# Token layers and last outputs of a scan network, put into one program order of rounds

## The chip, the cores and the metric

The kernel runs on one core of one Trainium2 chip. The metric is the device time of one execution, in microseconds (us). Five engines run at the same time, each with its own queue: TensorE (PE, matmuls and transposes into PSUM), VectorE (DVE), ScalarE (ACT), GpSimd (POOL), and SyncE (SP), which here only issues DMA transfers. They are synchronised by semaphores.

## What is computed

Four images of 64 x 64 positions (L = 4096 tokens) with 96 channels pass through four layers, all in float32 unless the layer quantises:

```python
# layers 0 and 1: selective scan over an image, four directions
xz = x @ in_proj_w.T;  xp, z = split(xz)
xc = silu(depthwise_conv3x3(xp) + conv_b)
# for each of 4 directions: delta, B, C from xc;  h = exp(delta*A)*h + delta*u*B;  y = C.h + D*u
y = layernorm(sum of the directions) * silu(z)
x = x + y @ out_proj_w.T
# layers 2 and 3: on tokens
x = x + attention(layernorm(x))    # no softmax: (q k^T) v, then @ Wff + bff
x = x + ffn(layernorm(x))          # 96 -> 384 -> 96, relu, fp8 (e5m2) products, fp16 accumulation rounding
```

Because the attention has no softmax, the kernel computes it as one 97 x 97 Gram matrix of the normalised tokens (with a column of ones), a chain of four small products that ends in a 97 x 96 matrix, and one product of the tokens with that matrix.

## The kernel before, in words

**Scans.** A scan layer treats the images in two pairs, so there are four units (layer 0 pair 0, layer 0 pair 1, layer 1 pair 0, layer 1 pair 1). A unit is a stage between scans (`between_scans`) and a scan (`PairScan.run`). The scan fills nearly all of the time. The stage between scans runs the input half of the next unit (projection, convolution, `Inputs`) together with the output half of the unit before (layer norm, gate, output projection, `Outputs`); the first stage has inputs only. It goes in beats, with `fill()` between the parts of a beat handing out pieces of the convolution to DVE, PE and POOL by `CONVS` and `SHARES`. `beginnings` is a generator that makes the first projection and first step sizes of the scan that follows; from beat 4 (first stage) or 8 (joined stages) on, four of its pieces are taken at the end of a beat. These stages and the scans use `InOrder`, a wrapper that fixes the order of compute instructions on each engine to the order in which the program writes them.

**Last outputs and token layers.** After the last scan, `token_layers` has two jobs: the `Outputs` of the last unit (16 groups of 256 positions for images 2 and 3, `one_by_one`), and the two token layers of all four images. Images 0 and 1 are already complete in DRAM and are loaded into `tok0` and `tok1` at once; `tok2` and `tok3` are loaded when the outputs are done.

- An output group g is loaded (`zt`, `xr`, three `ys` transfers), measured on DVE (`ystats`, `ymv`), turned into scale factors by a power on POOL (`ln_ve`, `ln_rs`) and a product on DVE (`shift`), normalised on ACT (`ys`), transposed on PE (`pt`), scaled back on ACT (`gt`), gated on DVE, projected on PE (`po`), copied on ACT (`xo`) and stored. All nine steps of a group are written one after the other. Loads have three buffers.
- A token norm (`token_norm`) takes statistics of 32 tiles of 128 tokens on DVE (`tstats`), combines them, takes the power -0.5 on POOL (`tn_ve`, `tn_rs`), forms `tshift` on DVE and applies scale and shift, three tiles of four on ACT and the fourth on POOL (`tn`).
- Attention: for each of 8 groups of 512 tokens, four matmuls into `gram`, four transposes (`tnps`) and an ACT copy to `tnt`; then the chain of small products; then for each group four matmuls (`ops`) and an addition to the tokens on DVE.
- ffn: for each of 8 groups, four transposes and a copy to fp8 (`xq`), three matmuls (`hps`), each followed by a copy to fp16 on ACT (`h`), bias and relu on DVE (`hb`) and a cast to fp8 on POOL (`hq`); then twelve matmuls (`ops`), a copy on ACT (`o`) and two additions on DVE.

Each image is a Python generator that yields between groups; a loop takes one step of the outputs and one step of every started image in turn, and image b may start at turn 13 b. In this stage the instructions are written through `tc.nc` and not through `InOrder`: the compiler's scheduler, which has a priority by the order of writing and its own estimate of durations, decides each engine's order. SP's order is the scheduler's before and after the change. PSUM is shared by tags with two buffers each: `tp` (transposes), `mm` (hidden products and the outputs' `pt`), `o` (outer products and the outputs' `po`).

Of the kernel before, what the change touches and what calls it, by code (L numbers as in the profile page):

```python
# [38 lines left out]
NT = L // 128  # L39
HID = 4 * C  # L40
# [23 lines left out]
def rstd_of(nc, pool, var, shape, tag, half):  # L64

    ve = pool.tile(shape, F32, name=f"{tag}_ve")
    nc.gpsimd.tensor_scalar(ve, var, EPS, None, ALU.add)
    rs = pool.tile(shape, F32, name=f"{tag}_rs")
    nc.gpsimd.tensor_tensor(rs, ve, half, ALU.pow)
    return rs  # L70
# [56 lines left out]
def between_scans(tc, cst, ident, half, pn, u, before, scan, after):  # L127

    with ExitStack() as stage:
# [16 lines left out]
        for beat in range(-LEAD, BEATS + 1):  # L146
# [4 lines left out]
            def fill():  # L151
                if beat < BEATS:
                    for one in convs:
                        one.go(ready)
# [18 lines left out]
            if now:  # L173
                outs.turn(beat)
            fill()
# [11 lines left out]
            if beat >= BEGIN[joint]:  # L187
                for _ in range(4):
                    next(beginnings, None)
# [18 lines left out]
    False: {'vector': ((0, 0, 16), (2, 0, 16), (0, 16, 16), (2, 16, 16), (0, 32, 16), (2, 32, 16), (2, 48, 16), (0, 48, 16)), 'tensor': ((1, 0, 8), (1, 8, 8), (1, 16, 8), (1, 24, 8), (1, 32, 8), (1, 40, 8), (1, 48, 8), (1, 56, 8))},  # L208
# [149 lines left out]
class Outputs:  # L358

    def __init__(self, nc, tc, stage, cst, ident, half, pn, layer, pr, pp, turned="pt", summed="po"):  # L360
# [8 lines left out]
        self.loaded, self.scaled, self.gated, self.sums = {}, {}, {}, {}  # L369
# [51 lines left out]
    def turn(self, g):  # L421
        nc, par, (_, _, ys) = self.nc, self.layer.par, self.loaded[g]
        self.gated[g] = gt = self.p2.tile([128, 3, 2, 128], F32, name="gt", bufs=2)
        for s, js, firsts in ((0, slice(0, 2), (0, 256)), (1, slice(2, 3), (128,))):
            pt = self.pp.tile([128, len(firsts), 2, 128], F32, name="pt", tag=self.turned)
            for j, first in enumerate(firsts):
                for t in range(2):
                    nc.tensor.transpose(pt[:, j, t], ys[:, t, first : first + 128], self.ident)
            nc.scalar.activation(
                gt[:, js], pt, AF.Identity, bias=par[:, s, P_NB : P_NB + 1], scale=par[:, s, P_NW : P_NW + 1]  # L430
            )
# [45 lines left out]
    def one_by_one(self):  # L477
        for g in range(BEATS):
            self.load(g)
            self.measure(g)  # L480
            self.scale(g)
            self.shift(g)
            self.normalise(g)
            self.turn(g)
            self.gate(g)
            self.project(g)
            self.store(g)
            yield
        self.close()
# [369 lines left out]
def token_norm(nc, pool, half, t, tn):  # L859

    stats = pool.tile([128, NT, 6], F32, name="tstats")
    for j in range(NT):
        nc.vector.bn_stats(stats[:, j], t[:, j])
        if j % 8 == 7:
            yield

    (m0, q0), (m1, q1) = ((stats[:, :, i], stats[:, :, i + 1]) for i in (1, 4))

    def small(name):
        return pool.tile([128, NT], F32, name=name)  # L870

    mean2, dev, var = small("tmean2"), small("tdev"), small("tvar")
    nc.vector.tensor_tensor(mean2, m0, m1, ALU.add)
    nc.vector.tensor_tensor(dev, m0, m1, ALU.subtract)
    nc.vector.scalar_tensor_tensor(dev, dev, 0.25, dev, ALU.mult, ALU.mult)
    nc.vector.tensor_tensor(var, q0, q1, ALU.add)
    nc.vector.scalar_tensor_tensor(var, var, 1.0 / C, dev, ALU.mult, ALU.add)
    rs = rstd_of(nc, pool, var, [128, NT], "tn", half)
    shift = small("tshift")
    nc.vector.scalar_tensor_tensor(shift, mean2, -0.5, rs, ALU.mult, ALU.mult)  # L880
    yield
    for j in range(NT):
        scale, bias = rs[:, j : j + 1], shift[:, j : j + 1]
        if j % 4 == 3:
            nc.gpsimd.tensor_scalar(tn[:, j, :C], t[:, j], scale, bias, ALU.mult, ALU.add)
        else:
            nc.scalar.activation(tn[:, j, :C], t[:, j], AF.Identity, bias=bias, scale=scale)
        if j % 8 == 7:
            yield

def turn_tokens(nc, pp, ident, tn, g, out):

    n = out.shape[0]
    ps = pp.tile([n, 512], F32, name="tnps", tag="tp")
    for j in range(4):
        nc.tensor.transpose(ps[:, 128 * j : 128 * j + 128], tn[:, 4 * g + j, :n], ident)
    nc.scalar.activation(out[:, 512 * g : 512 * g + 512], ps, AF.Copy, saturate=False)
# [8 lines left out]
def attention(nc, pool, pp, cst, ident, half, t, w):  # L906

    def product(a, b, name):

        ps = pp.tile([a.shape[1], b.shape[1]], F32, name=name, tag="small", bufs=1)  # L910
        nc.tensor.matmul(ps, a, b, start=True, stop=True)
        return ps

    def kept(ps, name):
        to = pool.tile(list(ps.shape), F32, name=name)
        nc.vector.tensor_copy(to, ps)
        return to

    tn = pool.tile([128, NT, C + 1], F32, name="tn", bufs=3)
    nc.gpsimd.memset(tn[:, :, C : C + 1], 1.0)  # L920
    yield from token_norm(nc, pool, half, t, tn)
    gram = pp.tile([C + 1, C + 1], F32, name="gram", bufs=1)
    tnt = pool.tile([C + 1, L], F32, name="tnt")
    for g in range(NT // 4):
        for j in range(4 * g, 4 * g + 4):
            nc.tensor.matmul(gram, tn[:, j], tn[:, j], start=(j == 0), stop=(j == NT - 1))
        turn_tokens(nc, pp, ident, tn, g, tnt)
        yield
    gk = kept(product(kept(gram, "gram_s"), w["wkv"][:, :C], "gkps"), "gk")
    vk = product(w["wkv"][:, C:], gk, "vkps")  # L930

    heads = pool.tile([C, C], F32, name="heads")
    nc.vector.tensor_tensor(heads, cst["heads"], vk, ALU.mult)
    rest = kept(product(heads, w["Wff"], "hps"), "rest")
    whole = pool.tile([C + 1, C], F32, name="whole")
    nc.vector.tensor_tensor(whole, w["bff"], product(w["wq"], rest, "wps"), ALU.add)
    yield
    for g in range(NT // 4):
        po = pp.tile([128, 4, C], F32, name="ops", tag="o")
        for j in range(4):  # L940
            at = 512 * g + 128 * j
            nc.tensor.matmul(po[:, j], tnt[:, at : at + 128], whole, start=True, stop=True)
        tg = t[:, 4 * g : 4 * g + 4]
        nc.vector.tensor_tensor(tg, tg, po, ALU.add)
        yield

def ffn_weights(nc, pool, w, n):

    def quantised(shape, src, name, back=False):
        raw = pool.tile(shape, F32, name=f"{name}{n}")  # L950
        nc.sync.dma_start(out=raw, in_=src)
        q = pool.tile(shape, E5M2, name=f"{name}q{n}")
        nc.vector.tensor_copy(q, raw, saturate=False)
        if back:
            nc.vector.tensor_copy(raw, q)
            return raw
        return q

    nh = HID // 128
    return (  # L960
        quantised([C, HID], w["W1"], "w1"),
        quantised([128, nh, C], w["W2"].rearrange("(k p) c -> p k c", p=128), "w2"),
        quantised([128, nh], w["b1"], "b1", back=True),
        quantised([128, 1, C], w["b2"].unsqueeze(0).partition_broadcast(128), "b2", back=True),
    )

def ffn(nc, pool, pp, ident, half, t, w, out=None):

    nh = HID // 128
    w1, w2, b1, b2 = w  # L970
    tn = pool.tile([128, NT, C + 1], F32, name="tn", bufs=3)
    yield from token_norm(nc, pool, half, t, tn)
    xq = pool.tile([C, L], E5M2, name="xq")
    for c in range(L // 512):
        turn_tokens(nc, pp, ident, tn, c, xq)
        yield
        cols = slice(512 * c, 512 * c + 512)
        hq = pool.tile([128, nh, 512], E5M2, name="hq")
        for k in range(nh):
            ps = pp.tile([128, 512], F32, name="hps", tag="mm")  # L980
            nc.tensor.matmul(ps, w1[:, 128 * k : 128 * k + 128], xq[:, cols], start=True, stop=True)
            h = pool.tile([128, 512], F16, name="h16")
            nc.scalar.copy(h, ps)
            hb = pool.tile([128, 512], F16, name="hb16")
            nc.vector.tensor_scalar(hb, h, b1[:, k : k + 1], 0.0, ALU.add, ALU.max)
            nc.gpsimd.tensor_copy(hq[:, k], hb, saturate=False)
        po = pp.tile([128, 4, C], F32, name="ops", tag="o")
# [5 lines left out]
        o = pool.tile([128, 4, C], F16, name="o16")  # L993
        nc.scalar.copy(o, po)
        ob = pool.tile([128, 4, C], F16, name="ob16")
        nc.vector.tensor_tensor(ob, o, b2.to_broadcast([128, 4, C]), ALU.add)
        tg = t[:, 4 * c : 4 * c + 4]
        nc.vector.tensor_tensor(tg, tg, ob, ALU.add)
        yield
# [200 lines left out]
```

## Time and profile before

| | |
|---|---|
| median of 3 runs | 10563.6 us (10562.44 to 10565.32) |
| the profiled execution: its own time, its span | 10567.09 us, 10565.3 us |
| last scan instructions on DVE and POOL | end at about 9918 and 9921 us |
| last-outputs and token stage | from about 9922 us to the end |
| its outputs: first statistics, last `xo` copy | 9955.5 us, 10061.8 us |
| busy over the span: PE, DVE, ACT, POOL | 76%, 91%, 84%, 88% |
| instructions of the span | 142182 |

The profile is one execution, recorded by the hardware profiler; times in it are counted from the span's start. A line of a group of instructions has the code line, engine, operation, output<-inputs, tile shapes and count, then the busy time, the mean duration in ns of one, and how long the engine stood idle just before them and for what. Many lines carry L60, the line of the wrapper `InOrder`; the tiles tell what they are. "PEclk" is the granted share of TensorE's full clock.

### The profile page before, as it was taken

How to read it: one execution, taken by the hardware profiler on the slowest of the kernel's cores; microseconds unless marked ns; L12 is line 12 of the kernel's file. 1: busy time of each engine (PE TensorE's matmuls, PEld its weight loads, DVE VectorE, ACT ScalarE, POOL GpSimd, SP SyncE). 2: the span in 40 equal slices, each digit the busy share in tenths (PEclk: the TensorE clock that was granted, in tenths of full speed). 3: DMA queues.
4: the chain of work that ended last, by engine and by line, in shares of the span. 5: the costliest groups of instructions: out<-in, count | busy, mean ns of one | idle time of the engine just before them, and what ended most of it. 6: DMA issues, size and time to landing. Idle time of an engine off the chain costs nothing.

```text
span 10565.3 us, 142182 instructions
## 1 busy us (share of the span) xinstructions
PE 8004.7 (76%) x47518; PEld 5948.7 (56%) x47518; DVE 9628.9 (91%) x6714; ACT 8827.3 (84%) x18798; POOL 9337.2 (88%) x5482
## 2 busy tenths in 40 slices
PE   7777777777777777777777777777877777777666
PEld 4655555554555555555455555555555555555554
DVE  7999999998999999998999999999899999999755
ACT  6888888887888888888888888888788888888756
POOL 3999999998999999998899999999799999999645
PEclk9889898988888889898889888888888998898877
DMA  4677777776667777777567777777566777777600
GB/s 138 202 215 219 218 217 219 221 219 173 206 212 212 217 218 219 219 218 215 169 208 215 214 215 221 223 215 220 172 207 210 215 218 216 218 219 219 197 22 25
DMA packets 903380, 2117.25 MB, mean 200 GB/s; under 512 B 330326, under 2 KB 639896, under 8 KB 704920
## 3 DMA queue, kind: packets, MB, share of 16 engines
q1 hardware_dynamic: 902648, 2108.15, 68.0%
q8 instruction: 378, 6.19, 0.3%
q14 instruction: 354, 2.90, 0.1%
HBM read 1946.42 MB, written 161.48 MB: 200 GB/s over the span
## 4 chain that ended last, share of the span: by engine, by line
ACT 34%; PE 18%; issue 18%; DVE 17%; POOL 10%; DMA 1%; SPq 0%; DVEq 0%; POOLq 0%; ACTq 0%
ACT x L60 15%; ACT da L60 12%; DVE h L60 10%; PE yp L60 6%; POOL h L60 6%; PE bp L60 5%; DVE bp L60 4%; ACT bp L60 2%; DVE u L60 1%; PE xps L60 1%; POOL dbu L60 1%; PE dps L60 1%; ACT L60 1%; PE dups L60 1%; DMA cb<-crow 1%
## 5 line engine op out<-in xcount | busy, mean ns | idle before, releaser
L60 POOL TENSOR_TENSOR h<-h,cb 128x1024 f32<-128x1024 f32 x3072 | 7194.5, 2366 | 231.3 <-issue 61.2
L60 DVE TENSOR_TENSOR_SCAN h<-da,last,bp 128x1024 f32<-128x1024 f32 x2064 | 4736.6, 2335 | 146.0 <-PE bp L60 22.4
L60 ACT ACTIVATE x<-dut,bt 128x128 f32<-128x128 f32 x12288 | 3495.0, 370 | 1.2 <-PE bp L60 1.1
L60 PE MATMUL yp<-ident,h 128*128 128x128 f32 x24576 | 3365.4, 297 | 10.2 <-POOL h L60 10.2
L60 PEld LDWEIGHTS yp<-ident,h 128*128 128x128 f32 x24576 | 3191.2, 156 | 126.8 <-issue 76.9
L60 ACT ACTIVATE da<-delta,amat 128x1024 f32<-128x1024 f32 x2752 | 3059.7, 1138 | 99.0 <-DVE h L60 97.0
L60 PE MATMUL bp<-ident,x 128*128 128x128 f32 x10240 | 1673.3, 315 | 1292.5 <-DVE h L60 950.6
L60 PEld LDWEIGHTS bp<-ident,x 128*128 128x128 f32 x10240 | 1355.8, 162 | 1849.0 <-ACT x L60 1012.3
L60 DVE TENSOR_TENSOR bp<-du,bp 128x1024 f32<-128x1024 f32 x1472 | 1780.3, 1213 | 269.9 <-PE bp L60 268.2
L60 DVE TENSOR_TENSOR_SCAN h<-da,bp 128x1024 f32<-128x1024 f32 x688 | 1537.8, 2274 | 49.0 <-ACT da L60 6.7
L60 PE MATMUL bp<-bparts,sel 96*128 96x512 bf16 x2944 | 917.2, 397 | 762.0 <-DVE h L60 745.6
L60 PEld LDWEIGHTS <-sel 96*128 96x128 bf16 x2944 | 226.0, 100 | 1559.2 <-DVE h L60 1042.8
L60 ACT ACTIVATE bp<-delta,amat 128x1024 f32<-128x1024 f32 x320 | 358.1, 1119 | 528.8 <-DVE h L60 527.1
L60 POOL TENSOR_TENSOR dbu<-du,bb 128x1024 f32<-128x1024 f32 x320 | 754.9, 2359 | 0.0
L60 DVE TENSOR_TENSOR_SCAN h<-bp,last,dbu 128x1024 f32<-128x1024 f32 x240 | 558.8, 2328 | 14.4 <-POOL dbu L60 13.2
L60 PE MATMUL xps<-u,wx 128*76 128x512 f32 x768 | 554.1, 810 | 0.0
L60 POOL COPY last<-h 128x2 f32<-128x2 f32 x1152 | 216.0, 188 | 339.8 <-DVE h L60 310.7
L60 ACT ACT_TABLE_LOAD x392 | 502.9, 1283 | 11.4 <-DMA x<-xo 4.5
L60 POOL TENSOR_TENSOR du<-delta,u 128x1024 f32<-128x1024 f32 x188 | 496.8, 2642 | 0.0
L60 PE MATMUL dps<-cdt,wdt 12*128 12x512 f32 x768 | 442.9, 657 | 0.0
L60 ACT COPY ysum<-yp 128x1024 f32<-128x1024 f32 x192 | 194.3, 1012 | 291.6 <-PE yp L60 291.6
L60 ACT COPY dut<-dups 128x512 f32<-128x512 f32 x384 | 220.2, 575 | 238.2 <-PE dups L60 238.2
(157 smaller groups left out, 6465.7 us busy)
## 6 DMA issues: line engine op xcount, KB each, us to landing
cb<-crow SPq DMA_DIRECT2D x1024, 1024.0 KB
cb<-crow SPq DMA_DIRECT2D x1024, 512.0 KB
bb<-crow SPq DMA_DIRECT2D x384, 256.0 KB
bb<-crow SPq DMA_DIRECT2D x128, 512.0 KB
y<-ysum SPq DMA_DIRECT2D x192, 256.0 KB
kept<-y SPq DMA_DIRECT2D x160, 256.0 KB
y<-ysum SPq DMA_DIRECT2D x64, 512.0 KB
zt<-zg SPq DMA_DIRECT2D x64, 384.0 KB
```

Of the source, the lines that this page charges most:

```text
L60: return self.tc.keep_in_program_order(getattr(self.engine, op)(*args, **kwargs))
```

## The change

Four parts.

1. In the stages between scans, a power's small preparation (`ve = var + EPS`) is on DVE and not on POOL; one piece of `beginnings` is taken at each `fill()` and no longer four at the end of a beat; in the first stage the convolution piece (1, 56, 8), 8 rows, is DVE's and not PE's. `turn` is split into the transposes and `scaled_back`, the two ACT copies, which follow at once.
2. The token stage uses `InOrder`: its compute instructions stay in the order of writing.
3. The order of writing is by rounds. A class `Rounds` collects tasks for numbered rounds; one step of the loop runs one round of the outputs and one round of every started image. A consumer is put at least one round after its producer. The outputs' groups are two rounds apart, with the load four rounds before the measurement. An image's attention groups are two rounds apart, its ffn groups three. A norm's statistics are taken behind the additions of the layer before; `tshift` comes several rounds after the power. Images start at rounds 0, 26, 52 and 77. Five rounds of the outputs are written ahead of the token loads and weights, and the weights' casts are moved to round 20 of image 0.
4. Buffers: `h` and `hb` 6, `hq` 8, `tn` 4, `xq` 3, `tnt` 2, `o` 4; the Gram matrices of the four images have one PSUM tile (`grams`), the small products another (`small`). `tok2` and `tok3` use the SBUF that the outputs leave.

```diff
+STARTS = (0, 26, 52, 77)
...
-    nc.gpsimd.tensor_scalar(ve, var, EPS, None, ALU.add)
-    rs = pool.tile(shape, F32, name=f"{tag}_rs")
+    nc.vector.tensor_scalar(ve, var, EPS, None, ALU.add)
+    rs = pool.tile(shape, F32, name=f"{tag}_rs", bufs=4)
     nc.gpsimd.tensor_tensor(rs, ve, half, ALU.pow)
...
             def fill():
+                if beat >= BEGIN[joint]:
+                    next(beginnings, None)
...
-            if beat >= BEGIN[joint]:
-                for _ in range(4):
-                    next(beginnings, None)
...
     def one_by_one(self):
+        rounds = Rounds()
         for g in range(BEATS):
...
+            for r, task in enumerate((
+                self.load, None, None, None, self.measure, self.scale, self.shift, self.normalise, self.turn,
+                self.scaled_back, self.gate, self.project, self.store,
+            )):
+                if task:
+                    rounds.at(2 * g + r, task, g)
+        yield from rounds.run()
...
+class Rounds:
+    def __init__(self):
+        self.tasks = {}
+    def at(self, r, task, *args):
+        self.tasks.setdefault(r, []).append((task, args))
+    def run(self):
+        for r in range(max(self.tasks) + 1):
+            for task, args in self.tasks.get(r, ()):
+                task(*args)
             yield
...
+# attention, from round `start` of its image
+    at(start, begin)                                  # norm.finish: tshift
+    for g in range(groups):
+        at(start + 1 + 2 * g, norm.apply, 4 * g, 2)
+        at(start + 2 + 2 * g, norm.apply, 4 * g + 2, 2)
+        at(start + 4 + 2 * g, turn, g)                # gram and transposes
+        at(start + 5 + 2 * g, lambda g: norm.keep(g, tiles["tnt"]), g)
+    chain = start + 2 * groups + 4                    # small products, rounds chain to chain + 8
...
+    for g in range(groups):
+        at(chain + 9 + 2 * g, outer, g)
+        at(chain + 10 + 2 * g, add, g)
+        at(chain + 11 + 2 * g, then.take, g)          # statistics of the next norm
+    end = chain + 11 + 2 * groups
+    at(end - 1, then.combine)                         # power on POOL
+    return end + 1 + 2
...
+# ffn
+    at(start, begin)
+    first = start + 6
+    for g in range(groups):
+        r = first + 3 * g
+        at(r - 5, norm.apply, 4 * g, 2)
+        at(r - 4, norm.apply, 4 * g + 2, 2)
+        at(r - 2, norm.turn, pp, ident, g)
+        at(r - 1, lambda g: norm.keep(g, tiles["xq"]), g)
+        for k in range(nh):
+            at(r + k, hidden, g, k)                   # PE
+            at(r + k + 1, rounded, g, k)              # ACT
+            at(r + k + 2, positive, g, k)             # DVE
+            at(r + k + 3, quantise, g, k)             # POOL
+        at(r + 7, outer, g)                           # PE
+        at(r + 8, round_out, g)                       # ACT
+        at(r + 9, add, g)                             # DVE
+        if then is not None:
+            at(r + 10, then.take, g)
+    end = first + 3 * groups + 8
...
+        nc = InOrder(tc)
...
+        for _ in range(5):
+            next(outs)
         load(0)
         load(1)
...
-            if begun < NB and turns >= 13 * begun and (begun < 2 or outs is None):
+            if begun < NB and turns >= STARTS[begun] and (begun < 2 or outs is None):
```

The words after # in this diff are added here for the reader; `CONVS[False]` moves the tuple (1, 56, 8) from its list for `tensor` to the end of its list for `vector`.

## The prediction

> **What bounds the kernel now.** I read the page's slices first, to see which stage the change sits in and how full the engines are there. The columns are 40 equal slices of 264 us.
>
> ```profile
> DVE  7999999998999999998999999999899999999755
> ACT  6888888887888888888888888888788888888756
> POOL 3999999998999999998899999999799999999645
> PEclk9889898988888889898889888888888998898877
> DMA  4677777776667777777567777777566777777600
> ```
>
> Up to slice 37 DVE and POOL are full: these are the scans, whose code does not change. In the last two slices and a half every engine falls to 4 to 7 tenths and TensorE's clock falls too. That is the stage that the change rewrites (last outputs plus token layers). Its stretches, from the table of busy time by window (us of window, then PE, PEld, DVE, ACT, POOL busy, the clock, DMA share, GB/s):
>
> ```profile
> 9922.00:9944.00 22.00, 0.00 (x0) 0.00 (x0) 7.18 (x46) 0.87 (x1) 0.55 (x4) 0.52 0.59 172
> 9944.00:10062.00 118.00, 84.69 (x627) 77.40 (x627) 50.36 (x213) 80.01 (x176) 38.99 (x52) 0.82 0.59 160
> 10062.00:10559.00 497.00, 335.45 (x2351) 258.34 (x2350) 285.55 (x946) 305.93 (x705) 265.89 (x337) 0.74 0.04 17
> ```
>
> The stage takes 10565.3 - 9922 = 643 us, and its busiest engine by a fixed clock, ACT, works 386.8 us of it (60%). In the third row no engine passes 68%, and DMA is idle. So no engine bounds the stage: engines wait for each other. The table of waits for 9922 to 10566 (waiter, what it waited for, us in total, times, longest) says on whom:
>
> ```profile
> POOL hq L986 <- DVE hb L985: 165.9, 133, 13.0
> PE ops L990 <- POOL hq L986: 110.9, 81, 11.4
> DVE tshift L880 <- POOL tn_rs L69: 92.0, 16, 8.1
> ACT tn L887 <- DVE tshift L880: 80.6, 6, 29.5
> ACT o L994 <- PE ops L990: 59.9, 37, 8.4
> ```
>
> Two patterns. Inside an ffn group PE, ACT, DVE, POOL, PE follow one another and each waits for the one before. And at each of the 16 token norms POOL computes one power of 5.5 us, DVE waits for it (16 times), and ACT, behind DVE, stood up to 29.5 us. The groups in that window give the durations (busy, mean ns):
>
> ```profile
> L887 ACT ACTIVATE tn<-tok,tshift,tn_rs 128x96 f32<-128x96 f32 x384 | 144.1, 458 | 80.6 <-DVE tshift L880 80.6
> L986 POOL CAST hq<-hb 128x512 fp8e5<-128x512 f16 x192 | 131.1, 690 | 195.4 <-DVE hb L985 165.9 <-PE gram L926 10.1 <-PE hps L981 8.8
> L69 POOL TENSOR_TENSOR tn_rs<-tn_ve,half 128x32 f32<-128x32 f32 x16 | 88.2, 5514 | 1.0
> ```
>
> **What the Trainium skill says.** Perfetto Trace Analysis, Per-engine timelines: ACT, DVE and GpSimd run their queues strictly first in, first out. The 80.6 us in six ACT waits agree: one tn at the head held everything behind it. So the order in which instructions are queued decides this stage, and the change is a new order. TensorE: Matmul & The Clock Gate, Part 1: the PE clock halves after about 3.4 us of idleness. The trace agrees: 0.50 in 10060 to 10100, 1.00 in 10000 to 10040, 0.74 over the third stretch; a steadier PE should run faster. GPSIMD Engine Reference, 1. Specifications: its SBUF interfaces are shared with VectorE. The trace agrees: the 128x4 ln_ve on POOL takes 1196 ns (median) between scans, beside DVE's convolution, and 228 ns in the token stage. ScalarE: Activation LUTs, Table sets: copies lie in every table set; the window indeed has no table load, so mixing ACT's tasks costs none.
>
> **The change part by part.** Durations are of the profiled execution (span 10565.3, its own time 10567.1, against the median of 10563.6); I work in the span and move the result onto the median.
>
> *Before the token stage.* (1) In the first stage 8 rows of convolution go from PE to DVE. PE runs its convolution back to back to 159.7 us and the first scan matmul starts at 160.5, so 9 matmuls x 0.43 us = 3.9 us come off the path; DVE gains 9 x 0.66 us (half of its 1.31 us for 128x1024) = 5.9 us, in the idle time that it has from 144.9 on. (2) ln_ve moves from POOL to DVE: 48 x 1.2 us = 57 us off POOL and some 48 x 0.2 = 10 us onto DVE, in three joined stages where DVE is 81 to 90% busy and both hold the path by turns. I take 2 us of gain for each stage, bounds -8 and +4. (3) The first projection of a scan is issued one piece per fill in place of four per beat: same instructions, up to two beats earlier, and not last in the stage (conv and the last outputs are): 0, bounds -3 and +3 per stage. Sum about -8, bounds -35 and +15.
>
> *The outputs.* SP now issues the loads of output groups 0 to 2 ahead of the 16 weight loads. Both orders begin with the two token images (3.1 MB from 9918, landed about 9933). The weights held SP from 9924.0 to 9941.9, and the first statistics on an output (ystats) came at 9955.5; now group 0 can be there at about 9937. But the 18 us of weight issues then lie between group 2 and group 3, so group 3 is issued at about 9962. Each group moves zt 384, xr 192, ys 384 and xo 192 KB = 1.18 MB, at the 217 GB/s seen in 10000 to 10040 5.4 us; 13 groups take 70 us and the last one's chain some 15: outputs end at 9962 + 85 = 10047, against 10062. Gain 15. Work hidden below: ACT needs 73 us for it and for image 0's first attention.
>
> *The token layers.* The same matmuls, copies and norms, now in rounds. An image lasts 191 rounds (statistics 10, attention 50, ffn 42, attention 50, ffn 39) and starts at 0, 26, 52, 77, so 268 in all; outputs take the first 38. I laid ACT's, DVE's, POOL's and PE's times on the rounds that the code gives. A price is a group's busy time by its count (0.36 us for a tn is the pitch in a run of seven, 2.51 us in the chain of waits); PE's group sums, in which neighbours overlap, are scaled by 0.8 to its busy time: per ffn group ACT has 3 x 0.36 + 0.59 + 3 x 0.56 + 0.48 = 3.8 us in 3 rounds, POOL 3 x 0.68 + 0.47, DVE 3 x 0.47 + 1.22 + 0.72, PE at the present mixed clock about 2.6; per attention group ACT 1.7 us in 2 rounds and PE 1.1, and later PE 0.6 and DVE 1.3 in 2 rounds.
>
> | rounds | images | PE | ACT | DVE | POOL | sum of each round's longest engine | taken |
> |---|---|---|---|---|---|---|---|
> | 38-77 | 1 to 2 | 34 | 38 | 34 | 26 | 64 | 51 |
> | 77-191 | 4 | 169 | 213 | 203 | 167 | 327 | 262 |
> | 191-243 | 3 to 2 | 56 | 67 | 63 | 52 | 108 | 83 |
> | 243-268 | 1 | 15 | 20 | 18 | 14 | 35 | 32 |
>
> The two ends for the time after round 38 are ACT's own 338 us (engines slide freely against each other) and 534 us (rounds act as barriers). A consumer one round behind has about a round of slack, so I go nearer to the low end. Rounds with one or two images: 64 x 1.3 us = 83, which is ACT's 3.8 us over 3 rounds and covers one hop. Rounds 191 to 243: 52 x 1.6 = 83. Heavy rounds: ACT's 213, plus 10 powers x 5.5 us of which half is not covered (a power holds POOL's casts; PE's second matmul comes two rounds after the last cast, about 4 us of slack, and powers of images 0 and 2, and 1 and 3, lie 1 to 2 rounds apart, at 148/150 and 174/175) = 27, plus 22 for uneven rounds = 262. Sum 428. The norm's wait itself goes: DVE's tshift stands four rounds behind the power, over 6 us. What is late next is ACT, then DVE.
>
> Then 10047 + 428 + 6.5 (the last store, 10558.8 to 10565.3 now) - 8 = 10473.5, 92 below the span: **about 10472 us** at the median.
>
> **The rivals.**
> - *Rounds as barriers (slower).* Each round costs its longest engine, because buffers of two (mm, tp, o in PSUM) pull the producer back as well: outputs 118 us by the same sum (9940 to 10058), then 534 us, +6.5 - 8 = 10590.5, +25: 10589. It decides from a mean of 2.29 us per round over the 227 rounds after the outputs; my forecast is 1.88, this rival 2.35. For it: rounds are uneven, 327 against 213 in the heavy part. Against it: six h and hb buffers, eight hq, four tn.
> - *Free flow.* ACT alone bounds: 10047 + 338 - 1.5, about 10384, median 10382. For it: PE's 335 us after the outputs would shrink towards 335 x 0.74 = 248 at full clock. Against it: single-image ends.
> - *Outputs held at DVE's head.* measure(g+3) sits on DVE in the round in which group g is gated, and waits for a ys load that can only start when group g is turned, two rounds before; behind it wait image 0's tasks. At 8 us a group (two slow rounds) the outputs end at 9937 + 128 + 10 = 10075, +28: 10500.
> - *Powers uncovered.* All of the 14 powers after the outputs at full price, 77 us for 27: 10522.
> - *Does not do what it says.* SP is not bound to program order: in the built queue ys loads of several groups run ahead of zt and xr. If that order is bad it ends in the third rival.
>
> **How the numbers follow.** Forecast 0.54, free flow 0.10, late outputs 0.12, uncovered powers 0.10, barriers 0.14. Range 10390 to 10580: below it lies most of free flow, above it most of barriers. A measurement here can tell about 0.2% (21 us) from no change: faster means under 10542, slower over 10585. Forecast, flow and nearly all of the two middle rivals are faster: 0.80; a bad mixture of the middle ones is within: 0.07; barriers: 0.13.
>
> **What would show it.** In the profile after: ystats of the last stage starts near 9937, outputs end (last xo) near 10047; the token stretch has ACT above 75% busy, PEclk above 0.8; the waits of tshift for tn_rs and of ACT for tshift are near zero; hq's wait for hb falls below 60 us. The first scan matmul comes near 156.5 us. I am wrong if ACT stays near 60% (barriers), if outputs end after 10070, or if the stages between the scans move by over 15 us together.

## The result, and the profile after

The changed kernel takes **10457.7 us** (median of 4 runs, 10455.2 to 10459.9), the kernel before beside it 10564.5 us: ratio 0.9897, 95% interval 0.988 to 0.9914. The forecast was 10472. The time is close, but the two parts of the change went differently from what the sum had: the token stage gained more, and the stages between the scans lost.

I read both traces at the same landmarks, by the starts of instructions: the last `ysum` copy of a scan is its end, the first `skip` copy on ACT is the start of the next one's output.

| | before | after | predicted change | measured change |
|---|---|---|---|---|
| first stage, start to first skip | 166.2 us | 164.6 us | | -1.6 |
| three joined stages | 190.9, 191.0, 187.3 | 201.4, 202.8, 190.6 | | +25.6 |
| four scans, code unchanged | 9186.5 | 9178.6 | 0 | -7.9 |
| end of the last scan | 9921.9 | 9938.0 | -8 | **+16.1** |
| outputs: from there to last `xo` | 139.9 | 119.6 | -15 | -20.3 |
| after it, to the end | 503.5 | 397.3 | -69 | **-106** |

The scans' scatter is a limit of this study: over the executions profiled here their sum lies between 9166 and 9197 us. Small edits are therefore read at the stages' landmarks and not at the whole time. These agree better: the eight executions profiled with the changed stages have 164.5 to 166.3 us in the first one and lie within 1.4 us of each other in each joined one. So the -1.6 of the first stage is not clear of the scatter; the +25.6 of the joined ones is.

The slices of the page, now 261 us each:

```profile
DVE  8999999999999999999899999999899999999957
ACT  6888888887888888888788888888788888888868
POOL 3999999997899999999699999999789999999946
PEclk9898998988888998888888989898988898988978
DMA  4677777776577777777477777777757777777730
```

The ragged end is shorter: one slice of 5, 6 and 4 (the outputs, in which DMA is 65% busy, as the next table shows), then one of 7, 8 and 6. POOL dips to 7, 6 and 7 in slices 10, 20 and 29, two of them deeper than before (8, 8 and 7): these are the joined stages, relieved of `ln_ve`. They did not get shorter for it. The stretches of the last stage (us of window, then PE, PEld, DVE, ACT, POOL busy, clock, DMA share, GB/s):

```profile
9938.00:9950.00 12.00, 0.00 (x0) 0.00 (x0) 0.00 (x0) 0.99 (x1) 0.00 (x0) 0.54 1.05 321
9950.00:10058.00 108.00, 73.27 (x520) 67.24 (x520) 56.37 (x269) 66.94 (x144) 32.36 (x27) 0.77 0.65 175
10058.00:10448.00 390.00, 284.56 (x2456) 240.61 (x2456) 271.78 (x966) 309.12 (x737) 255.76 (x334) 0.84 0.06 22
```

In the third row ACT is busy 309 of 390 us, 79% for 62% before, with the same work, and the clock rose from 0.74 to 0.84. The waits of the stage (waiter, what it waited for, us in total, times, longest), 9938 to 10455:

```profile
POOL hq L61 <- DVE hb L61: 88.3, 83, 4.2
...
PE ops L61 <- POOL hq L61: 46.2, 21, 6.0
ACT o L61 <- PE ops L61: 39.7, 14, 6.8
...
DVE ystats L61 <- DMA ys<-y: 32.9, 14, 15.1
DVE tshift L61 <- POOL tn_rs L61: 32.7, 12, 5.4
```

All five pairs shown of before shrank: hq from 165.9 to 88.3, PE's wait for hq from 110.9 to 46.2, tshift from 92.0 to 32.7, o from 59.9 to 39.7, and ACT's tn from 80.6 to 17.5. Two things are left. POOL's wait for hb is 83 short waits of 1 us, slack of an engine that isn't full. PE's and ACT's are few and long, up to 6.0 and 6.8 us, a little over the length of one power (5.53 us). The groups (busy, mean ns):

```profile
L61 ACT ACTIVATE tn<-tok,tshift,tn_rs 128x96 f32<-128x96 f32 x384 | 164.5, 485 | 23.3 <-DVE tshift L61 17.5 <-issue 5.8
L61 POOL CAST hq<-hb 128x512 fp8e5<-128x512 f16 x192 | 122.7, 650 | 92.1 <-DVE hb L61 88.3 <-PE grams L61 2.3 <-PE ops L61 1.3
...
L61 POOL TENSOR_TENSOR tn_rs<-tn_ve,half 128x32 f32<-128x32 f32 x16 | 88.5, 5530 | 45.1 <-DVE tn_ve L61 35.4 <-ACT tn L61 5.5 <-ACT xq L61 2.5
```

Counts are those of before and durations within 7%: the work is the same; what changed is its order, its buffers, and that `ve` is on DVE here too, since all norms share one helper.

### The profile page after: what moved, and what is told of

Its sections match the earlier page's. It is cut to its first block, busy times and chain, and to the rows that moved or that the text cites. A ratio compares the mean times of both kernels' runs of the same rounds, so it can differ in the third digit from the quotient of the medians.

```text
span 10454.9 us, 142148 instructions
## 1 busy us (share of the span) xinstructions
PE 7920.4 (76%) x47500; PEld 5900.9 (56%) x47500; DVE 9648.0 (92%) x6803; ACT 8817.8 (84%) x18798; POOL 9255.7 (89%) x5402
## 4 chain that ended last, share of the span: by engine, by line
ACT 34%; issue 20%; DVE 17%; PE 16%; POOL 11%; DMA 2%; SPq 1%; DVEq 0%; POOLq 0%; ACTq 0%
ACT x L61 14%; ACT da L61 12%; DVE h L61 9%; POOL h L61 8%; PE yp L61 6%; PE bp L61 5%; DVE bp L61 4%; ACT bp L61 2%; DVE u L61 1%; PE xps L61 1%; POOL dbu L61 1%; DMA cb<-crow 1%; PE dps L61 1%; ACT L61 1%; PE dups L61 1%
## 5 line engine op out<-in xcount | busy, mean ns | idle before, releaser
L61 DVE TENSOR_TENSOR_SCAN h<-bp,last,dbu 128x1024 f32<-128x1024 f32 x240 | 558.9, 2329 | 13.4 <-POOL dbu L61 12.7
```

What stands on the lines that cost most here:

```text
L61: return self.tc.keep_in_program_order(getattr(self.engine, op)(*args, **kwargs))
```

## The experiments

"Token stage" is from the last ysum to the end: 643.4 us before, 516.9 after, and 513.7 to 517.0 in the four other runs that leave the token stage as changed. "Stages" are the first and the three joined ones.

### One half of the change at a time

`e1_tokens_only` undoes part 1 (conv piece, spread beginnings, ve on DVE in the stages between scans); `e2_between_only` does part 1 alone, on the token stage of before.

```diff
-    nc.vector.tensor_scalar(ve, var, EPS, None, ALU.add)      # e1: on POOL between scans
+    (on or nc.vector).tensor_scalar(ve, var, EPS, None, ALU.add)
-                if beat >= BEGIN[joint]:                      # e1: out of fill()
-                    next(beginnings, None)
+            if beat >= BEGIN[joint]:                          # e1: four at the end of a beat
+                for _ in range(4):
+                    next(beginnings, None)
...
-    nc.gpsimd.tensor_scalar(ve, var, EPS, None, ALU.add)      # e2, against before; `on` is DVE between scans
+    (on or nc.gpsimd).tensor_scalar(ve, var, EPS, None, ALU.add)
```

Both have the tuple (1, 56, 8) of `CONVS[False]` moved as well, e1 back to `tensor`, e2 to `vector`.

> The changed kernel with the three edits between the scans undone (ve on POOL, pieces of the beginnings four at the end of a beat, all of the first stage's eight rows on PE). By landmarks the part ahead of the token stage took 16 us longer in the changed kernel (last ysum copy at 9938.0 against 9921.9). If that comes from these three edits, and not from the token stage, this kernel ends about 16 us earlier than the changed one: 10442 us, with the last ysum copy back at 9922. If the 16 us are an accident of the run, it stays at 10458.

Measured: 10438.8 us, ratio 0.988 (0.9865 to 0.9895); stages 166.1; 191.4, 191.0, 186.4; token stage 516.9.

> The kernel before with only the three edits between the scans. If the two halves of the change add up: 10564 + 16 = 10580 us, with the last ysum copy at 9938 and a token stage of 643 us. If the edits cost only in company with the new token stage: 10564.

Measured: 10578.6 us, ratio **1.0017** (1.001 to 1.0024); stages 165.3; 201.4, 202.0, 191.0; token stage 642.8.

The halves don't touch each other. Part 1 by itself makes the kernel slower, by 0.17% (0.10 to 0.24), which is 18 us between the means and 15 between the medians; the whole gain is in the stage behind the last scan.

### Which edit between the scans costs

`e3_old_beginnings` is the changed kernel with four pieces of beginnings at the end of a beat; `e4_ve_on_pool` is the changed kernel with ve on POOL between scans; `e15_conv_only` does both, so that of part 1 only the convolution piece is left. Their edits are those of the diff above: e4 the one of ve, e3 the two of beginnings, e15 all three.

> The changed kernel with the pieces of the beginnings taken four at the end of a beat again; ve stays on DVE. Theory A (PE blocked at its head: the projection's transposes now stand on PE before DVE has made rest, parts and du, two waits of about 7 us in the first joined stage): 10458 - 16 = 10442 us. Theory B (ve on DVE delays a DVE that is 86% busy): no change, 10458.

> The changed kernel with ve on POOL again in the stages between the scans alone; the beginnings stay spread. Theory A (PE blocked at its head): 10458 us, no change. Theory B (ve on DVE): 10442 to 10446 us.

> The changed kernel with two of its three edits between the scans undone: ve in the stages between scans back on POOL, and beginnings again four pieces at the end of a beat; the eight rows of convolution stay on DVE, the token stage stays as changed. From the runs so far: ve on DVE costs about 8 us in each of the first two joined stages and 1 to 3 in the third, spread beginnings about 8 in the first stage and 2 to 3 in each joined one, the moved convolution gains 9.5 in the first. If these add, the first stage takes 156.6 us and the joined ones 191, 191 and 187 (changed kernel: 164.6; 201.4, 202.8, 190.6), and the time is 34 us below the changed kernel's 10458, near 10424, give or take the 8 us by which the scans vary. If the effects do not add (each edit pays only beside another), a joined stage stays above 195 and the time above 10440.

| conv on DVE | beginnings | ve on | run | first | joined | time |
|---|---|---|---|---|---|---|
| no | four | POOL | before | 166.2 | 190.9, 191.0, 187.3 | 10564.5 |
| yes | spread | DVE | after | 164.6 | 201.4, 202.8, 190.6 | 10457.7 |
| yes | four | DVE | e3 | 156.6 | 198.7, 198.8, 191.0 | 10430.6 |
| yes | spread | POOL | e4 | 165.3 | 193.5, 193.9, 190.1 | 10442.0 |
| yes | four | POOL | e15 | 157.7 | 191.1, 191.2, 186.9 | 10427.4 |

(The first row has the token stage of before.) Line by line: the moved convolution gains 8.5 in the first stage (e15 against before); ve on DVE costs 7.6, 7.6 and 4.1 in the joined stages (e3 against e15); spread beginnings cost 7.6 in the first stage and 2.4, 2.7 and 3.2 in the joined ones (e4 against e15). The effects add within 1.3 us, but for the last joined stage: its terms sum to 194.2, and the changed kernel has 190.6. There spreading costs 3.2 us with ve on POOL and nothing with ve on DVE (190.6 against 191.0 in e3); the reason is open.

**Why ve costs.** DVE's groups in the first joined stage of e3 have the row that the prediction had set at 0.2 us an instruction:

```profile
L61 DVE TENSOR_SCALAR ln_ve<-ymv 128x4 f32<-128x4 f32 x16 | 12.7, 797 | 0.5
```

It is 797 ns in the mean, and DVE's timeline (start, duration) shows two kinds:

```profile
2470.47 1.63 DVE L61 TENSOR_SCALAR ln_ve<-ymv 128x4 f32<-128x4 f32 x1
...
2495.89 0.17 DVE L61 TENSOR_SCALAR ln_ve<-ymv 128x4 f32<-128x4 f32 x1
```

POOL's timeline has the reason beside it:

```profile
2470.26 1.81 POOL L61 TENSOR_TENSOR gt<-gt,zt 128x768 f32<-128x768 f32 x1 [7.95 <-ACT gt L61]
...
2496.14 1.98 POOL L61 TENSOR_TENSOR ln_rs<-ln_ve,half 128x4 f32<-128x4 f32 x1 [0.48 <-DVE ln_ve L61]
```

The long one ends at 2472.10, just when POOL's gate product ends (2472.07); the short one runs while POOL is idle and waits for it. Seven of the 16 take 1.56 us or more, each beside a gate product and ending within 0.03 us of its end. This fits the sharing of SBUF interfaces for which the prediction cited the Trainium skill, GPSIMD Engine Reference, 1. Specifications, in the other direction: the small operation is slowed on either engine when the other works on a large one. The page limits the contention to certain VectorE instructions, and no run here shows whether `ln_ve` is one of them. The trace before had a sign of it, in `shift`, an operation of the same size on DVE in the same stage, which took 1.58 us at most:

```profile
L60 DVE SCALAR_TENSOR_TENSOR shift<-ymv,ln_rs 128x4 f32<-128x4 f32 x16 | 7.6, 475 | 1.5 <-POOL ln_rs L60 1.5
```

And of the two engines DVE is the fuller. The joined stage by window, before and e3 (PE, PEld, DVE, ACT, POOL):

```profile
2462.00:2653.00 191.00, 161.24 (x478) 83.43 (x478) 163.23 (x278) 142.69 (x248) 136.75 (x84) 0.86 0.53 159
```
```profile
2446.00:2645.00 199.00, 157.34 (x479) 82.81 (x478) 172.97 (x293) 142.66 (x248) 116.36 (x77) 0.87 0.51 150
```

POOL lost 20.4 us, DVE gained 9.7, and the stage grew by 7.8, with DVE idle for 28 us in the one and 26 in the other: the stage's length goes with DVE's work. The last joined stage agrees. There `shift` fell from 15.4 us to 11.1 when ve came to DVE, which offsets part of ve's 10.6, and the stage grew by only 4.1 (e15 and e3). A second cause was not tested apart: POOL's `ln_rs` now waits for DVE's `ln_ve`, 23.8 us in the first joined stage of e3.

**Why spreading costs.** DVE's timeline of the first stage, after:

```profile
93.01 3.90 DVE L61 SCALAR_TENSOR_TENSOR u<-img,par,u 128x1024 f32<-128x1024 f32 x3
106.72 0.42 DVE L61 TENSOR_TENSOR rest<-btps,parts 128x256 f32<-128x256 f32 x1 [9.81 <-ACT parts L61]
```

`rest` is a piece of beginnings. Taken earlier, it came to DVE's head before ACT had made its `parts`, and the convolution behind it stood for 9.8 us (9.8 in e4 as well, with ve on POOL). In e3 DVE goes from 92.8 to 103.8 without such a gap:

```profile
92.77 3.91 DVE L61 SCALAR_TENSOR_TENSOR u<-img,par,u 128x1024 f32<-128x1024 f32 x3
96.59 0.81 DVE L61 TENSOR_SCALAR u<-img,par 128x1024 f32<-128x1024 f32 x1
```

The last statistic of the stage (`mv`), for which PE's group norm waits, is there at 149.5 in place of 157.2. The same instructions, only earlier, and 7.6 us lost. For the 2 to 3 us in the joined stages no single wait was traced.

### Order, and the round between

`e5_free_order` writes the token stage in the same rounds with the same buffers, but leaves each engine's order to the compiler's scheduler. `e6_same_round` keeps the fixed order and takes the lag away: in a round an image's consumers follow their producers at once.

```diff
-        nc = InOrder(tc)                      # e5
+        nc = tc.nc
...
-            at(r + k + 1, rounded, g, k)      # e6, and likewise tnt, xq, outer, o, add, take
-            at(r + k + 2, positive, g, k)
-            at(r + k + 3, quantise, g, k)
+            at(r + k, rounded, g, k)
+            at(r + k, positive, g, k)
+            at(r + k, quantise, g, k)
```

> The changed kernel with the token stage written in the same rounds but through tc.nc: the compiler's scheduler orders each engine again. In the changed kernel the stage from the last ysum copy to the end lasts 517 us, in the one before 643. Theory C (it is the fixed order, consumer a round behind, that takes the waits away): most of the gain goes, a stage of 580 to 643 us, 10520 to 10580 in all. Rival (the rounds as order of writing, with the new buffers, are enough for the scheduler): 517 +- 15 us, 10458.

Measured: 10501.7 us, ratio 0.9937 (0.9922 to 0.9952); token stage 560.9.

> The changed kernel with the lag taken out: in attention and ffn a consumer is put into the round of its producer (copy with the transposes, copy, relu and cast with the hidden product, second product, copy and addition with the last cast), order still fixed, same number of rounds. Theory C (the lag hides the chain): PE stands at each second product for copy, relu and cast, about 0.6 + 0.4 + 0.65 us and three wake-ups, near 2 us for each of 64 groups, part of it beside ACT's work: stage 560 to 640 us, 10500 to 10580 in all. Rival (a fixed interleaving of four images is enough, the lag adds nothing): 517 +- 10 us, 10458.

Measured: 10704.6 us, ratio **1.0127** (1.011 to 1.0144); token stage 767.8. The stage is far above the 560 to 640 us expected. Its waits, 9937 to 10705:

```profile
POOL hq L61 <- DVE hb L61: 271.8, 130, 8.7
...
PE ops L61 <- POOL hq L61: 204.7, 133, 6.7
ACT o L61 <- PE ops L61: 194.9, 64, 7.8
DVE ob L61 <- ACT o L61: 192.7, 64, 7.7
```

So of the 126 us the new order of writing, with all else that changed in this stage (buffers, order of loads, ve on DVE), gives 82 even through the scheduler (643.4 to 560.9), and fixing the order gives 44 more. PE's wait for hq shrinks in the same two steps: 110.9 us before, 79.8 in e5, 46.2 after. What makes up the 82 was not separated: the old order of writing with the new buffers was not run. A fixed order without the lag is worse than before by 124 us: each of the 64 ffn groups (8 in each of 4 images and 2 layers) makes ACT wait for PE and DVE for ACT once (the counts of 64 in the last two lines; `ob` is the first of DVE's two additions), and other images' tasks stand behind.

### What a power costs

`e7_double_power` takes each token norm's power twice; `e14_no_power` puts a multiplication of the same shape in its place (0.37 us for 5.53); `e13_power_pieces` cuts it into four pieces in consecutive rounds. What the power would cost on DVE stays open: `e9_power_dve`, which was to put it there, gave no time.

```diff
+        ve = self.pool.tile([128, NT], F32, name="tn_ve2", bufs=2)     # e7: once more
+        nc.vector.tensor_scalar(ve, var, EPS, None, ALU.add)
+        nc.gpsimd.tensor_tensor(self.rs, ve, self.half, ALU.pow)
...
-    nc.gpsimd.tensor_tensor(rs, ve, half, ALU.pow)                      # e14
+    nc.gpsimd.tensor_tensor(rs, ve, half, ALU.pow if tag == "ln" else ALU.mult)
...
+    def power(self, q):                                                 # e13, q = 0 to 3
+        cols = slice(8 * q, 8 * q + 8)
+        self.nc.gpsimd.tensor_tensor(self.rs[:, cols], self.ve[:, cols], self.half[:, cols], ALU.pow)
```

> The changed kernel with each token norm's power computed a second time on POOL (16 x 5.5 = 88 us more on POOL, same result). If the four rounds between power and tshift cover it and POOL has room (256 us busy of 390): +0 to 15 us. My forecast's price (half uncovered): about +44 us. If every power stands in the path: +88 us, 10546.

Measured: 10548.6 us, ratio 0.9977 (0.9968 to 0.9985); token stage 610.1, +93.2 for 88 us of POOL.

> The changed kernel, but the power of the token norms is left out: a multiplication of the same shape stands in its place, so the tokens are not normalised; the layer norm of the outputs keeps its power. This measures what the 16 powers of 5.53 us (88 us of POOL) cost in the changed kernel. The prediction let 10 powers in the heavy rounds cost 27 us and those in light rounds lie in the 1.3 us of a round. The chain after the outputs holds tn_rs for 38 us. If a power costs only what the chain shows: the token stage falls from 516.9 by about 38, to 479. If its full price is on the path, as the second power's was (93 for 88): by about 80, to 437. If a power is covered once, and only a second one was not: by less than 15.

Measured: 10407.3 us, ratio 0.9852 (0.9837 to 0.9867); token stage 459.5, -57.4 for 82.6 us of POOL; behind the outputs 344.1 us against 397.3. The window of e14 behind its outputs, and two of its waits:

```profile
10058.00:10396.00 338.00, 269.48 (x2456) 227.22 (x2456) 271.78 (x966) 306.90 (x737) 186.60 (x327) 0.91 0.06 25
```
```profile
ACT o L61 <- PE ops L61: 8.1, 7, 2.8
...
PE ops L61 <- POOL hq L61: 4.5, 7, 1.1
```

PE's wait for hq falls from 46.2 us to 4.5 and ACT's for PE from 39.7 to 8.1: those few long waits were the powers, holding POOL's casts. The waits of tshift for the power fall too, from 32.7 to 0.2, and how the 57 us split between the two was not measured. The first copy of a power costs 0.7 of its length, the second 1.06; the second also outlasts the rounds kept free for it, since in e7 tshift waits 117.0 us.

> The changed kernel, but each token norm's power (128x32, 5.53 us on POOL) is written as four powers of 128x8 in four consecutive rounds; tshift keeps its distance of two to four rounds behind the first. The total of POOL's work rises (128x4 takes 1.03 us, 128x32 5.46 us between scans: about 1.66 us for 128x8, 6.6 us a norm, 18 us in all). The run with the power taken twice gave its full price, 93 us for 88 us. Theory A: what a power costs is the blocking of POOL's queue: casts stand behind it, and PE's second product behind them. Then pieces let the casts through, and the token stage falls from 516.9 us by 10 to 30. Theory B: POOL's total work counts (it is the engine whose time sets the rounds): the stage rises by about 18. Theory C: the latency from the statistics to tshift counts: pieces in later rounds make it longer by up to three rounds, 14 norms x up to 3 us, and the stage rises by 10 to 40.

Measured: 10482.6 us, ratio 0.9924 (0.9907 to 0.994); token stage 535.6, **+18.7**. Its waits, 9938 to 10473:

```profile
DVE tshift L61 <- POOL tn_rs L61: 77.1, 16, 8.1
...
ACT tn L61 <- DVE tshift L61: 55.3, 15, 9.0
...
PE ops L61 <- POOL hq L61: 26.5, 22, 2.6
```

Theory A's mechanism is there, since PE's waits fell from 46.2 to 26.5 us and the longest from 6.0 to 2.6. It was more than paid for: the pieces take 107.6 us of POOL for 88.5, and as the last piece comes three rounds later (one round later for an image's first norm) under an unmoved tshift, DVE's and ACT's waits rose by 44 and 38 us. How much of the 18.7 is POOL's 19 us and how much is latency stays open; pieces with tshift moved as well were not run.

### Weights between the loads, and other starts

`e11_weights_later` moves the 16 weight loads out from between the outputs' third and fourth group. `e16_starts` is e15_conv_only with `STARTS = (0, 22, 45, 67)`.

```diff
-        nc.sync.dma_start(out=tiles[name], in_=w[name])                 # e11
+        waiting.append(lambda to=tiles[name], of=w[name]: nc.sync.dma_start(out=to, in_=of))
...
+                for i, one in enumerate(waiting):
+                    rounds.at(4 + i, one)
```

> The changed kernel, but the 16 weight loads are no longer issued between the outputs' third and fourth group: they go one by one into rounds 4 to 19 of image 0, the weights' casts to round 26. In the changed kernel the outputs' phase (last ysum copy to last xo copy) is 119.6 us and everything behind it 397. My theory: the 18 us of weight issues on SP hold group 3 back by as much, and the outputs end by that much later. Then the phase falls by 10 to 15 us, to about 105 to 110, the time by about 10. Rival 1: the phase is set by image 0's rounds (ACT and PE work of a round) and not by the loads: within 3 us. Rival 2: the weight loads now fall between the later groups' loads, one in each round, and hold each up a little: the hole comes back in pieces, within 3 us or worse by up to 5.

Measured: 10458.8 us, ratio 0.9899 (0.9884 to 0.9914); outputs' phase 115.0 for 119.6, token stage 513.1. DVE's wait for the outputs' loads:

```profile
DVE ystats L61 <- DMA ys<-y: 33.9, 18, 6.0
```

The one long wait is gone (15.1 us after, now 6.0 at most), and the total is what it was, 33.9 for 32.9: the hole comes back in pieces, as rival 2 had it. The 4.6 us of the phase are no more than e14 and e4, which leave these loads where they were, also show (115.4 and 116.5).

> The run e15_conv_only (10427, token stage 513.7) with one edit more: the images start at rounds 0, 22, 45 and 67 in place of 0, 26, 52 and 77. An image's powers come in its rounds 8, 56, 98 and 148; with the old starts eight of the 16 fall into pairs of two images 1 to 4 rounds apart (56/60, 82/85, 148/150, 174/175), with the new ones most stand 2 to 5 apart, but none within 2 except as before none share a round, and the whole has 258 rounds for 268. Theory A: of the 53 us that the powers cost behind the outputs, part comes from pairs that hold POOL for 11 us at a stretch, and ten rounds fewer save 10 x 1.3 us at the ends: the stage falls by 10 to 20, the time to about 10412. Theory B: the work of the dense rounds sets the time (ACT 309 us of 390) and each power costs what it costs wherever it stands: fewer rounds only make the rounds fuller, and the stage stays within 5. Theory C: image 2 starts seven rounds behind the outputs' end and its tokens, 3.1 MB with image 3's, are not there: the engines stand at its first statistics, and the stage rises by 5 to 15.

Measured: 10427.9 us, ratio 0.9875 (0.9858 to 0.9891); token stage 515.6 against 513.7 in e15. This is as theory B had it: there are ten rounds fewer, and each is fuller. In the rounds behind the outputs ACT is busy 80% in both.

**The best version** is e15_conv_only, 10427.4 us (ratio 0.9868, 0.9853 to 0.9883): 30 us below the changed kernel, and 137 below before. By time alone it can't be told from e3_old_beginnings and e16_starts; the landmarks tell it from e3, by 18 us over the four stages.

## Why the prediction was right, and where it was wrong

The sum ended at a span of 10473.5; it was 10454.9, 18.6 less. By its terms: +24.1 before the token stage, -5.5 in the outputs, -37.2 behind them. Two misses of opposite sign stand behind a close time, so its closeness is in part luck. (The terms before the token stage also add up to -9.9, and the sum carried -8.)

- **The convolution piece: right, but half the size.** -3.9 predicted, -8.5 measured. The term counted 9 matmuls; PE's convolution matmuls of the first stage went from 144 to 126. In the code the piece is nine matmuls, but the trace records each as two: the eight pieces before are 72 in the code and 144 in the trace. So it was 18, and 18 x 0.43 = 7.7.
- **ve on DVE: wrong sign.** -2 per joined stage predicted, +7.6, +7.6 and +4.1 measured. The failed step is "some 48 x 0.2 = 10 us onto DVE": the price was that of the operation alone. It was to be read off the trace before, where `shift`, of the same 128x4 on DVE in the same stage, took 475 ns in the mean and 1.58 us at most. "Both hold the path by turns" finds no support either: the stage grew although POOL lost 20 us.
- **Spread beginnings: wrong.** 0 (within 3) predicted; +7.6 in the first stage, 2.4 to 3.2 in the others. The argument was "same instructions, earlier, and not last in the stage". It left out that an instruction issued earlier also waits earlier, at the head of a queue that is strictly first in, first out (the Trainium skill, Perfetto Trace Analysis, Per-engine timelines; here `rest`, 9.8 us). The marker that stages moving by over 15 us together would make me wrong did apply, and the first scan matmul came at 159.5 and not near 156.5; with the beginnings of e3 it came at 151.5.
- **Outputs: right.** Gain 15 predicted, 20 measured. The first ystats came 12.7 us behind the last scan's end (15 in the sum, 33.6 before), and from there to the last xo it took 106.9 us for 106.3 before, so the whole gain is the earlier beginning. The hole of the weights was there (15.1 us). The last xo came at 10057.6 and not at 10047, because the scans ended 16.1 us later. That the hole itself cost something is not borne out: e11 without it gained nothing.
- **Token rounds: right mechanism, two terms off.** 428 us predicted for 227 rounds, 390 measured, 1.72 us a round for 1.88. Powers were set at 27 us: e14 measures 53 behind the outputs. The prediction's four rounds of distance (two for an image's first norm) keep tshift from waiting long, 5.4 us at most, but not the casts, which stand behind the power on POOL for longer than PE's slack. Without powers the rounds take 338 us (344.1 less the last store's 6.5), where the sum had 401. So the allowances for uneven rounds (22) and for light rounds at 1.3 us were far too large. That 338 is also the free-flow rival's sum of ACT's own work is chance in part: ACT's busy time there is 307 us (91%), so that sum was some 30 us too high.
- **Rivals.** Rounds as barriers did not come (it was to decide from 2.29 us a round, and 1.72 came), but e6 shows how much chains of waits can cost: without the lag the whole stage costs 767.8. Outputs held at DVE's head did not come: from the first ystats to the last xo the 16 groups took 6.7 us each and not 8. SP did issue loads of several groups out of the written order (nine ys transfers in a row at 9970), and the outputs still ended in time. Free flow was near on the rounds and left the powers out; the powers' 53 us lie half-way between the forecast's 27 and the 77 of the rival that leaves them uncovered.
- **Markers.** ACT above 75% (79%) and the clock above 0.8 (0.84): met. The reason given for the clock is not borne out, though. In the trace before it fell to 0.50 at about 10050 us, where PE had stood idle for 2.2 us at most since 10020, and stayed there through 80 matmuls in a row (10061.5 to 10078.8). So the 3.4 us of idleness that the prediction quoted do not explain this fall, and its cause stays open. Waits for tn_rs and tshift near zero: 32.7 and 17.5, not met. hq's wait below 60: 88.3, not met, and a bad marker, since POOL waits there because it has little to do: in e14, the fastest stage, it is 97.5.

## What to carry to other kernels

Where several independent chains share in-order engines, write consumers a round behind producers and fix that order; here a fixed order without the lag was worse than leaving the order to a scheduler. Before moving a small instruction from one engine to another, take its price from a neighbour of the same size on the target engine in the same stage, and ask which of the two engines the stage's length follows. An instruction moved earlier is free only if its inputs are there earlier as well; otherwise it stops everything behind it.

## What the runs showed of the hardware that I had not expected

A 128x4 operation on DVE takes 0.17 us beside an idle POOL and up to 1.66 us beside POOL's large elementwise products, ending with them; at 16 such in a stage this made 12.7 us of what looked like 3. And a power's price on POOL grows less than its size: 128x8 takes 1.69 us, 128x32 5.53, so four pieces of 8 columns cost 22% more than one of 32.
